# Paired bilinear products: x turned by disjoint pairs, part of w in place, five blocks of x through GpSimd's queue

## The chip, the cores and the metric

The kernel runs on one core of a Trainium2 chip. A core has a matrix engine (TensorE, PE), a vector engine (VectorE, DVE), a scalar engine (ScalarE, ACT), a general engine (GpSimd, POOL) and a queue engine (SyncE, SP). They share an on-chip memory of 128 partitions; PE writes its results to a second, small one, PSUM. Sixteen DMA engines move data between the on-chip memory and HBM; transfers are issued from the queues of SP, ACT and POOL.

The metric is the device time of one execution in microseconds (us), lower is better. The kernel before takes 1345.69 us, the median of 9 runs from 1344.93 to 1346.57.

## The reference

```python
# inputs: (4096, 32, 64) float32; W: (496, 64, 64) float32
idx_i, idx_j = np.triu_indices(F, k=1)      # the 496 pairs i < j of 32 fields
vi = inputs[:, idx_i, :]
vj = inputs[:, idx_j, :]
vidots = jnp.einsum('bpd,pde->bpe', vi, W)
return vidots * vj                          # (4096, 496, 64) float32
```

For each row of the batch and each pair (i, j), field i is multiplied by the pair's own 64x64 matrix and the result, element by element, by field j. The output has 520 MB; x has 33.6 MB and W 8.1 MB.

## The kernel before

**Tiles.** The 4096 rows form 16 blocks of 256; a block has two tiles of 128 rows, one row to a partition (two neighbouring rows of the batch share a partition, one for each tile). The list `steps` goes through the fields i, and for each i through its pairs in chunks of at most 16 (`CH`). The pairs are cut into five groups by `bounds`; a group's results for a tile are gathered in one tile `ot` of a pool of three buffers, and one SP transfer (L266) writes it to HBM, some 3 MB. The first group of the first tile goes out in two transfers.

**A step.** PE needs x with its elements across partitions. `turn_x` (L138) turns eight windows of two neighbouring fields each: window s holds fields s - 1 and s, so that each field comes up twice, once in each half of the partitions. ACT copies the result from PSUM to `xT` (L147, 128x1024). The matrices W are taken in two halves h of 32 columns: two matmuls (L244), one from each half of the partitions, fill the two banks of a tile `ps`. A step that crosses a bound of `wrows` (multiples of 128 pairs) needs two more. Then DVE multiplies `ps` by field j and writes `ot` (L261). For the first chunk of the fields in `aside`, ACT copies `ps` to `tmp` (L258) and POOL multiplies (L259).

**W.** It is loaded in four parts of 128, 128, 128 and 112 pairs (`load_w`, L113) to tiles `raw`. `order_w` (L120) sorts a quarter of a part on DVE, POOL or ACT into a tile `rp` of the pool that `tmp` uses, PE turns it (`turn_w`, L127), and ACT copies it to the part's own tile `wT`. The first two parts' `raw` use buffers of `ot`; parts three and four use, one after the other, a buffer of their own. Part four is loaded by ACT's queue after the last `order_w` of part three (L231).

**The order of the work.** It is written out in the program. The first three tiles (`LEAD`) go through the groups together, the others one by one (`sched`). The dictionary `due` puts turns of x four steps (`AHEAD`) before the step that needs them, and the work on W at fixed steps. In steps 52 to 66 (`no_aside`) no product goes to ACT and POOL.

**Loads of x.** SP loads block 0 in two halves, with W's first three parts and block 1 (L193 to L200). Later blocks are loaded one block ahead, into two buffers. `new_x` (L69) takes the buffer and has POOL clear one field at its front (L72). Then ACT's queue loads 128 rows of 16 KB (`load_x`), except for blocks 4, 7, 10 and 13: `load_fifteen` (L95) loads 120 rows by two transfers from POOL's queue, in pieces of 4 KB, and the last 8 rows by two transfers from ACT's queue (5 rows and 3). After each of POOL's two comes a transfer of 17 rows of a few bytes (`turn_engines`, L86); one of 5 rows stands at the start and one of 11 at the end.

Of the kernel before, what the change touches and what calls it, by code (L numbers as in the profile page):

```python
# [8 lines left out]
F32 = mybir.dt.float32  # L9
# [3 lines left out]
def kernel(  # L13
# [16 lines left out]
    nc = tc.nc  # L30

    B, F, D = x.shape
    P = 128
    NB = 2
    assert 2 * D == P and B % (NB * P) == 0
    NBLK = B // (NB * P)
    NP = F * (F - 1) // 2
    E2 = D // 2
    BANK = 512
    CH = BANK // E2  # L40
    RUN = 2 * BANK // P
    p0 = [i * (F - 1) - i * (i - 1) // 2 for i in range(F)]


# [4 lines left out]
    aside = (1, 3, 5, 7, 9, 11, 13)  # L49

    cuts = [*range(0, NP, P), NP]
    wrows = list(zip(cuts[:-1], cuts[1:]))

    const = ctx.enter_context(tc.tile_pool(name="const", bufs=1))
    xpool = ctx.enter_context(tc.tile_pool(name="xpool", bufs=2))
    xtpool = ctx.enter_context(tc.tile_pool(name="xtpool", bufs=4))
    tpool = ctx.enter_context(tc.tile_pool(name="tpool", bufs=4))
    opool = ctx.enter_context(tc.tile_pool(name="opool", bufs=3))
    psum = ctx.enter_context(tc.tile_pool(name="psum", bufs=4, space=bass.MemoryType.PSUM))

    ident = const.tile([P, P], F32, tag="ident", name="ident")
    make_identity(nc, ident)

    xs = {}

    def rows_of(dram: bass.AP, blk: int) -> bass.AP:
        return dram[blk * NB * P : (blk + 1) * NB * P]

    def new_x(blk: int):  # L69

        xs[blk] = xpool.tile([P, 1 + NB * F, D], F32, tag="xs", name=f"xs_{blk}")
        nc.gpsimd.memset(xs[blk][:, 0, :], 0.0)  # L72

    def load_x(blk: int, eng, k0: int = 0, k1: int = NB):
        src = rows_of(x, blk).rearrange("(p k) f d -> p (k f) d", k=NB)
        eng.dma_start(out=xs[blk][:, 1 + k0 * F : 1 + k1 * F, :], in_=src[:, k0 * F : k1 * F, :])

# [1 line left out]
    SWR = 120  # L81
# [4 lines left out]
    def turn_engines(k: int):  # L86
        n = k if k > 1 else 17
        c = used[0] % 8
        used[0] += 1
        src = x[: NB * n].rearrange("(p k) f d -> p k f d", k=NB)  # L90
        tc.keep_in_program_order(
            nc.gpsimd.dma_start(out=scratch[:n, :, c : c + 1], in_=src[:, :, 0, 0:1])  # L92
        )

    def load_fifteen(blk: int):  # L95
        rows = rows_of(x, blk).rearrange("(p k) f d -> p k f d", k=NB)
        dst = xs[blk][:, 1:, :].rearrange("p (k f) d -> p k f d", k=NB)
        for a, b in ((SWR, SWR + 5), (SWR + 5, P)):
            nc.scalar.dma_start(out=xs[blk][a:b, 1:, :], in_=rows[a:b].rearrange("p k f d -> p (k f) d"))
        for h in range(2):  # L100
            cut = slice(h * F // 2, (h + 1) * F // 2)
            tc.keep_in_program_order(
                nc.gpsimd.dma_start(out=dst[:SWR, :, cut, :], in_=rows[:SWR, :, cut, :])  # L103
            )
            turn_engines(1)


    wflat = w.rearrange("p d e -> p (d e)")
    raw, wT = {}, {}
    EU = 2 * BANK // P  # L110
    NU = E2 // EU

    def load_w(c: int, eng=nc.sync):  # L113

        a, b = wrows[c]
        pool, tag = ((opool, "ot"), (opool, "ot"), (const, "w3"), (const, "w3"))[c]
        raw[c] = pool.tile([P, D * D], F32, tag=tag, name=f"raw_{c}")
        eng.dma_start(out=raw[c][: b - a, :], in_=wflat[a:b])

    def order_w(c: int, k: int, copy):  # L120
        r = wrows[c][1] - wrows[c][0]
        rp = tpool.tile([P, EU, 2, D], F32, tag="tmp", name=f"rp_{c}_{k}")
        src = raw[c][:r, :].rearrange("p (d h e) -> p e h d", h=2, d=D)
        copy(rp[:r], src[:, k * EU : (k + 1) * EU])  # L124
        return rp

    def turn_w(c: int, k: int, rp, copy):  # L127
        r = wrows[c][1] - wrows[c][0]
        if c not in wT:
            wT[c] = const.tile([P, r, E2], F32, tag=f"w{c}", name=f"wT_{c}")  # L130
        pt = psum.tile([P, EU, P], F32, tag="ps", name=f"ptw_{c}_{k}")
        for n in range(EU):
            nc.tensor.transpose(  # L133
                pt[:, n, :r], rp[:r, n].rearrange("p h d -> p (h d)"), ident[:r, :r]
            )
        copy(wT[c][:, :, k * EU : (k + 1) * EU], pt[:, :, :r].rearrange("p e r -> p r e"))  # L136

    def turn_x(blk: int, k: int, q: int, copy):  # L138

        pt = psum.tile([P, RUN, P], F32, tag="ps", name=f"ptx_{blk}_{k}_{q}")  # L140
        for n in range(RUN):
            s = k * F + q * RUN + n
            nc.tensor.transpose(  # L143
                pt[:, n, :], xs[blk][:, s : s + 2, :].rearrange("p f d -> p (f d)"), ident
            )
        xT = xtpool.tile([P, RUN, P], F32, tag="xT", name=f"xT_{blk}_{k}_{q}")
        copy(xT, pt)  # L147
        return xT


# [8 lines left out]
    first = {}  # L159
# [11 lines left out]
    place = {ts: n for n, ts in enumerate(sched)}  # L171


    AHEAD = 4
    due: dict = {}
    for t in range(NT):
        for q in range(F // RUN):
            at = place[t, first[q * RUN - 1] if q else 0] - AHEAD
            due.setdefault(max(0, at), []).append(("x", t // NB, t % NB, q))
    for c, orders, turns in (  # L180
        (1, (2, 4, 8, 10), (4, 7, 12, 15)),
        (2, (17, 22, 27, 32), (19, 24, 29, 34)),
        (3, (54, 54, 55, 55), (57, 60, 63, 66)),
    ):
        for k in range(NU):
            due.setdefault(orders[k], []).append(("order", c, k))
            due.setdefault(turns[k], []).append(("turn", c, k))
    no_aside = range(52, 67)
    LATE = 6
    loads = {place[blk * NB, LATE]: blk + 1 for blk in range(2, NBLK - 1)}  # L190
    loads[place[LEAD, LATE]] = 2
# [3 lines left out]
    load_w(0)  # L195
    load_w(1)
    load_x(0, nc.sync, 1, NB)
    load_w(2)
    new_x(1)
    load_x(1, nc.sync)  # L200
    turn_engines(5)

    v, p, a = nc.vector.tensor_copy, nc.gpsimd.tensor_copy, nc.scalar.copy
# [9 lines left out]
    for s, (t, st) in enumerate(sched):  # L213
        blk, kt = divmod(t, NB)
        g, i, c0, m = steps[st]
        if s in loads:
            new_x(loads[s])
            if loads[s] % 3 == 1:
                load_fifteen(loads[s])
            else:  # L220
                load_x(loads[s], nc.scalar)
        for what, *args in due.get(s, ()):
            if what == "x":
                xT[tuple(args)] = turn_x(*args, a)
            elif what == "turn":
                turn_w(*args, rps.pop(tuple(args)), a)
            else:
                c, k = args
                rps[c, k] = order_w(c, k, (v, v, p, v)[c] if k % 2 == 0 else (v, v, p, a)[c])
                if (c, k) == (2, NU - 1):  # L230
                    load_w(3, nc.scalar)  # L231

        base, end = groups[g]
        pa = p0[i] + c0
        if pa == base:
            ots[t] = opool.tile([P, cap, D], F32, tag="ot", name=f"ot_{t}_{g}")
        ot = ots[t]
        ps = psum.tile([P, 2, CH, E2], F32, tag="ps", name=f"ps_{s}")
        for c, (lo, hi) in enumerate(wrows):
            lo, hi = max(pa, lo), min(pa + m, hi)  # L240
            if lo < hi:
                for h in range(2):
                    n = i + 1 - h
                    nc.tensor.matmul(  # L244
                        ps[:, h, lo - pa : hi - pa, :],
                        xT[blk, kt, n // RUN][h * D : (h + 1) * D, n % RUN, :],
                        wT[c][h * D : (h + 1) * D, lo - wrows[c][0] : hi - wrows[c][0], :],
                        start=True,
                        stop=True,
                    )  # L250
        o = pa - base
        j = 1 + kt * F + i + 1 + c0
        dst = ot[:, o : o + m, :].rearrange("p m (h e) -> p m h e", h=2)
        src = ps[:, :, :m, :].rearrange("p h m e -> p m h e")
        xj = xs[blk][:, j : j + m, :].rearrange("p m (h e) -> p m h e", h=2)
        if i in aside and c0 == 0 and s not in no_aside:
            tmp = tpool.tile([P, CH, 2, E2], F32, tag="tmp", name=f"tmp_{s}")
            nc.scalar.copy(tmp, src)  # L258
            nc.gpsimd.tensor_mul(dst, tmp, xj)  # L259
        else:  # L260
            nc.vector.tensor_mul(dst, src, xj)  # L261

        ends = (p0[2], end) if s < NS and (t, g) == (0, 0) else (end,)
        if pa + m in ends:
            n0 = p0[2] if len(ends) > 1 and pa + m == end else base
            nc.sync.dma_start(  # L266
                out=rows_of(out, blk).rearrange("(p k) n d -> p k n d", k=NB)[:, kt, n0 : pa + m, :],
                in_=ot[:, n0 - base : pa + m - base, :],
            )
# [28 lines left out]
```

## Time and profile before

| | before |
|---|---|
| median of 9 runs | 1345.69 us |
| profiled execution: time, span | 1344.93 us, 1343.1 us |
| busy: PE, DVE, POOL, ACT | 1160.6, 956.2, 544.9, 374.1 us |
| moved by DMA | 562.95 MB, 419 GB/s on average |
| HBM read, written | 41.68 MB, 520.09 MB |
| median time from issue to landing: output transfers | 16.3 to 17.1 us |
| the same: x by ACT's queue, x by POOL's queue | 17.8, 31.5 us |
| mean granted clock of TensorE | 0.963 |

The span runs from the first instruction to the last on the core; the execution's time is a little longer. Busy time is the sum of an engine's instructions. In a row of a stretch of time, the columns are the stretch, its length, the busy time of PE, PE's weight loads, DVE, ACT and POOL (with counts), the granted clock, the mean busy share of the 16 DMA engines, and GB/s. In a row of waits, they are who waited for whom, the total in us, how often, and the longest.

### The profile page before, as it was taken

How to read it: one execution, taken by the hardware profiler on the slowest of the kernel's cores; microseconds unless marked ns; L12 is line 12 of the kernel's file. 1: busy time of each engine (PE TensorE's matmuls, PEld its weight loads, DVE VectorE, ACT ScalarE, POOL GpSimd, SP SyncE). 2: the span in 40 equal slices, each digit the busy share in tenths (PEclk: the TensorE clock that was granted, in tenths of full speed). 3: DMA queues.
4: the chain of work that ended last, by engine and by line, in shares of the span. 5: the costliest groups of instructions: out<-in, count | busy, mean ns of one | idle time of the engine just before them, and what ended most of it. 6: DMA issues, size and time to landing. Idle time of an engine off the chain costs nothing.

```text
span 1343.1 us, 17902 instructions
## 1 busy us (share of the span) xinstructions
PE 1160.6 (86%) x7424; PEld 677.1 (50%) x7424; DVE 956.2 (71%) x1262; ACT 374.1 (28%) x367; POOL 544.9 (41%) x264
## 2 busy tenths in 40 slices
PE   6989889888898888888889988888988889889894
PEld 4555545544455444455545554444554445545552
DVE  5778768766677677776757777576876667767774
ACT  3432322223232232222222322232222323223321
POOL 1822424444243445333444434442444424344431
PEclk9989999999999899998989999899899989989997
DMA  9999999999999999999999999999999999999997
GB/s 394 376 422 420 422 426 432 428 418 432 423 431 422 431 430 399 428 424 432 429 418 419 413 428 430 425 426 416 418 423 414 430 420 431 420 430 424 423 418 319
DMA packets 28258, 562.95 MB, mean 419 GB/s; under 512 B 3456, under 2 KB 3456, under 8 KB 5504
## 3 DMA queue, kind: packets, MB, share of 16 engines
q1 hardware_dynamic: 24048, 530.59, 93.0%
q10 hardware_dynamic: 1632, 23.33, 4.2%
q0 software_dynamic: 2496, 7.88, 1.5%
q8 instruction: 58, 0.95, 0.3%
q14 instruction: 24, 0.20, 0.0%
HBM read 41.68 MB, written 520.09 MB: 418 GB/s over the span
## 4 chain that ended last, share of the span: by engine, by line
DMA 52%; PE 22%; DVE 15%; POOL 6%; issue 2%; ACT 1%; DVEq 0%; SPq 0%; POOLq 0%; ACTq 0%
DMA out_dram<-ot 51%; PE ps L244 17%; DVE ot L261 15%; POOL ot L259 5%; PE ptx L143 4%; PE ptw L133 1%; DMA raw<-in_L_rec_W_dram 1%; POOL scratch L92 1%; ACT tmp L258 1%; POOL xs L103 0%; DVE rp L124 0%; POOL rp L124 0%; DVEq L261 0%; ACT wT L136 0%; POOL xs L72 0%
## 5 line engine op out<-in xcount | busy, mean ns | idle before, releaser
L261 DVE TENSOR_TENSOR ot<-ps,xs 128x1024 f32<-128x1024 f32 (+15 forms) x1252 | 944.9, 809 | 356.1 <-DMA out_dram<-ot 193.0
L244 PE MATMUL ps<-wT,xT 64*128 64x512 f32 (+13 forms) x6272 | 1015.6, 466 | 122.3 <-DVE ot L261 110.3
L244 PEld LDWEIGHTS ps<-wT,xT 64*128 64x128 f32 x6272 | 550.9, 193 | 552.7 <-DVE ot L261 291.0
L259 POOL TENSOR_TENSOR ot<-tmp,xs 128x1024 f32<-128x1024 f32 x220 | 519.3, 2361 | 621.0 <-ACT tmp L258 441.3
L258 ACT COPY tmp<-ps 128x1024 f32<-128x1024 f32 x220 | 222.8, 1013 | 465.9 <-PE ps L244 388.4
L147 ACT COPY xT<-ptx 128x1024 f32<-128x1024 f32 x128 | 129.6, 1012 | 453.6 <-PE ptx L143 453.6
L143 PE MATMUL ptx<-ident,xs 128*128 128x128 f32 x1024 | 141.2, 281 | 38.5 <-DVE ot L261 29.8
L143 PEld LDWEIGHTS ptx<-ident,xs 128*128 128x128 f32 x1024 | 111.1, 142 | 85.1 <-issue 42.2
L72 POOL MEMSET xs<- 128x64 f32 x16 | 2.4, 151 | 148.9 <-DVE ot L261 148.9
L133 PE MATMUL ptw<-ident,rp 128*128 128x128 f32 (+1 forms) x128 | 18.0, 292 | 3.9 <-DVE rp L124 3.9
L136 ACT COPY wT<-ptw 128x1024 f32<-128x1024 f32 (+1 forms) x15 | 14.8, 984 | 20.3 <-PE ptw L133 20.3
L133 PEld LDWEIGHTS ptw<-ident,rp 128*128 128x128 f32 (+1 forms) x128 | 15.1, 153 | 10.3 <-DVE rp L124 5.0
L124 DVE COPY rp<-raw 128x1024 f32<-128x1024 f32 (+1 forms) x9 | 10.7, 1217 | 11.2 <-DMA raw<-in_L_rec_W_dram 11.2
L92 POOL DMA_DIRECT2D scratch<-in_r_inputs_dram x10 | 9.1, 908 | 0.2 <-issue 0.2
L124 POOL COPY rp<-raw 128x1024 f32<-128x1024 f32 x4 | 7.9, 1981 | 0.1
L124 ACT COPY rp<-raw 112x1024 f32<-112x1024 f32 (+1 forms) x3 | 5.9, 1953 | 4.6 <-POOL ot L259 2.8
L103 POOL DMA_DIRECT2D xs<-in_r_inputs_dram x8 | 6.0, 753 | 1.4 <-issue 1.4
L136 DVE COPY wT<-ptw 128x1024 f32<-128x1024 f32 x1 | 1.2, 1225 | 2.4 <-PE ptw L133 2.4
L147 ACT ACT_TABLE_LOAD x1 | 1.3, 1283 | 0.7 <-PEq L285 0.7
masks.py:197 POOL MEMSET ident<- 128x128 f32 x1 | 0.2, 204 | 0.3 <-POOLq L285 0.3
masks.py:199 POOL TENSOR_SCALAR_AFFINE_SELECT ident<-ident 128x128 f32<-128x128 f32 x1 | 0.3, 287 | 0.0
L285 POOL MEMSET const-float32-0.0<- 128x1 f32 x1 | 0.1, 93 | 0.3 <-issue 0.3
(3 smaller groups left out, 0.3 us busy)
## 6 DMA issues: line engine op xcount, KB each, us to landing
out_dram<-ot SPq DMA_DIRECT2D x64, 3360.0 KB, 16.3
out_dram<-ot SPq DMA_DIRECT2D x32, 3168.0 KB, 16.4
out_dram<-ot SPq DMA_DIRECT2D x32, 3104.0 KB, 17.0
out_dram<-ot SPq DMA_DIRECT2D x31, 2880.0 KB, 17.1
xs<-in_r_inputs_dram ACTq DMA_DIRECT2D x10, 2048.0 KB, 17.8
xs<-in_r_inputs_dram POOLq DMA_DIRECT2D x8, 960.0 KB, 31.5
raw<-in_L_rec_W_dram SPq DMA_DIRECT2D x3, 2048.0 KB, 17.5
xs<-in_r_inputs_dram SPq DMA_DIRECT2D x2, 1024.0 KB, 5.5
```

Source lines behind the costliest of these rows:

```text
L72: nc.gpsimd.memset(xs[blk][:, 0, :], 0.0)
L92: nc.gpsimd.dma_start(out=scratch[:n, :, c : c + 1], in_=src[:, :, 0, 0:1])
L103: nc.gpsimd.dma_start(out=dst[:SWR, :, cut, :], in_=rows[:SWR, :, cut, :])
L124: copy(rp[:r], src[:, k * EU : (k + 1) * EU])
L133: nc.tensor.transpose(pt[:, n, :r], rp[:r, n].rearrange("p h d -> p (h d)"), ident[:r, :r])
L136: copy(wT[c][:, :, k * EU : (k + 1) * EU], pt[:, :, :r].rearrange("p e r -> p r e"))
L143: nc.tensor.transpose(pt[:, n, :], xs[blk][:, s : s + 2, :].rearrange("p f d -> p (f d)"), ident)
L147: copy(xT, pt)
L244: nc.tensor.matmul(ps[:, h, lo - pa : hi - pa, :], xT[blk, kt, n // RUN][h * D : (h + 1) * D, n % RUN, :], wT[c][h * D : (h + 1) * D, lo - ...
L258: nc.scalar.copy(tmp, src)
L259: nc.gpsimd.tensor_mul(dst, tmp, xj)
L261: nc.vector.tensor_mul(dst, src, xj)
```

## The change

Six things change together:

- `turn_x` turns eight fields by four disjoint windows of two fields, so a tile takes 16 transposes, not 32. ACT makes three copies of the result: all 128 partitions to the first half of `xT`, and each half of the partitions to the other half, in the second half of `xT`. The field at the front of a block's tile, and POOL's clearing of it, go. A block's tile now has 16 spare elements after each row, so ACT's loads come in pieces of 8 KB.
- The first three parts of W share one tile for 384 pairs (`home_of`); no step is split at 128 or 256 any more. The third part is loaded straight into its place in this tile and sorted from there.
- The fourth part of W is loaded by SP at the start, after block 1 and the third part. Block 1 now comes before the third part.
- Blocks 3, 6, 9, 12 and 15 go through POOL's queue: 120 rows in one transfer of 8 KB pieces, one of 17 short rows, then the last 8 rows in two transfers, each with half of the fields.
- x is turned six steps ahead, not four; W's third and fourth parts are sorted and turned at other steps.
- `no_aside` goes; in the first three tiles ACT copies `ps` to `ot` itself and POOL multiplies in place.

```diff
-    RUN = 2 * BANK // P
+    RUN = 8
...
-        xs[blk] = xpool.tile([P, 1 + NB * F, D], F32, tag="xs", name=f"xs_{blk}")
-        nc.gpsimd.memset(xs[blk][:, 0, :], 0.0)
+        wide = xpool.tile([P, NB, F * D + 16], F32, tag="xs", name=f"xs_{blk}")
+        xs[blk] = wide[:, :, : F * D].rearrange("p k (f d) -> p k f d", d=D)
...
-        for a, b in ((SWR, SWR + 5), (SWR + 5, P)):
-            nc.scalar.dma_start(out=xs[blk][a:b, 1:, :], in_=rows[a:b].rearrange("p k f d -> p (k f) d"))
+        def part(ps: slice, fs: slice):
+            tc.keep_in_program_order(nc.gpsimd.dma_start(out=dst[ps, :, fs, :], in_=rows[ps, :, fs, :]))
+
+        part(slice(0, SWR), slice(0, F))
+        turn_engines(1)
         for h in range(2):
-            cut = slice(h * F // 2, (h + 1) * F // 2)
-            tc.keep_in_program_order(
-                nc.gpsimd.dma_start(out=dst[:SWR, :, cut, :], in_=rows[:SWR, :, cut, :])
-            )
-            turn_engines(1)
+            part(slice(SWR, P), slice(h * F // 2, (h + 1) * F // 2))
...
+    def home_of(c: int):
+        home, tag, n = (wrows[3][0], "w3", NP - wrows[3][0]) if c == 3 else (0, "w", wrows[3][0])
+        if home not in wT:
+            wT[home] = const.tile([P, n, E2], F32, tag=tag, name=f"wT_{home}")
+        return wT[home][:, wrows[c][0] - home : wrows[c][1] - home, :]
...
+        if c == 2:
+            raw[c] = home_of(c).rearrange("p r e -> p (r e)")
...
-        for n in range(RUN):
-            s = k * F + q * RUN + n
+        for u in range(RUN // 2):
+            f = q * RUN + 2 * u
             nc.tensor.transpose(
-                pt[:, n, :], xs[blk][:, s : s + 2, :].rearrange("p f d -> p (f d)"), ident
+                pt[:, u, :], xs[blk][:, k, f : f + 2, :].rearrange("p f d -> p (f d)"), ident
             )
-        copy(xT, pt)
+        copy(xT[:, 0], pt)
+        copy(xT[D:, 1], pt[:D])
+        copy(xT[:D, 1], pt[D:])
...
-    AHEAD = 4
+    AHEAD = 6
...
-        (2, (17, 22, 27, 32), (19, 24, 29, 34)),
-        (3, (54, 54, 55, 55), (57, 60, 63, 66)),
+        (2, (16, 18, 25, 27), (30, 33, 36, 39)),
+        (3, (46, 48, 50, 52), (56, 59, 62, 65)),
...
-    load_w(2)
     new_x(1)
     load_x(1, nc.sync)
+    load_w(2)
+    load_w(3)
...
-            if loads[s] % 3 == 1:
+            if loads[s] % 3 == 0:
                 load_fifteen(loads[s])
...
-                if (c, k) == (2, NU - 1):
-                    load_w(3, nc.scalar)
...
-        if i in aside and c0 == 0 and s not in no_aside:
-            tmp = tpool.tile([P, CH, 2, E2], F32, tag="tmp", name=f"tmp_{s}")
+        if i in aside and c0 == 0:
+
+            tmp = dst
+            if t >= LEAD:
+                tmp = tpool.tile([P, CH, 2, E2], F32, tag="tmp", name=f"tmp_{s}")
```

## The prediction

> **What bounds the kernel now.** I read the page's slices first, then its chain of waits, then the stretches of the span where the transfer rate falls short.
>
> ```profile
> PE 1160.6 (86%) x7424; PEld 677.1 (50%) x7424; DVE 956.2 (71%) x1262; ACT 374.1 (28%) x367; POOL 544.9 (41%) x264
> ...
> DMA  9999999999999999999999999999999999999997
> ...
> q0 software_dynamic: 2496, 7.88, 1.5%
> ...
> DMA out_dram<-ot 51%; PE ps L244 17%; DVE ot L261 15%; POOL ot L259 5%; PE ptx L143 4%; PE ptw L133 1%; DMA raw<-in_L_rec_W_dram 1%; POOL scratch L92 1%; ACT tmp L258 1%; POOL xs L103 0%; DVE rp L124 0%; POOL rp L124 0%; DVEq L261 0%; ACT wT L136 0%; POOL xs L72 0%
> ```
>
> No compute engine is full; the 16 DMA engines are, in every slice but the last. The output transfers carry half of the chain. So the time is 563 MB over the rate, plus what the rate loses, and a change of compute is worth only what it does to the DMA. The second view, busy time by stretch, shows where rate is lost (last columns: DMA share, GB/s):
>
> ```profile
> 2.00:26.00 24.00, 14.56 (x82) 10.54 (x84) 10.97 (x11) 9.09 (x9) 2.64 (x2) 1.00 1.00 419
> 26.00:36.00 10.00, 10.00 (x58) 5.25 (x56) 8.51 (x9) 4.05 (x4) 3.85 (x3) 1.00 0.88 368
> 36.00:56.00 20.00, 20.00 (x122) 11.29 (x118) 14.64 (x15) 9.29 (x10) 16.42 (x9) 1.00 0.95 404
> 56.00:64.00 8.00, 8.00 (x56) 5.20 (x56) 5.41 (x6) 4.09 (x5) 5.88 (x3) 1.00 0.99 318
> 64.00:92.00 28.00, 23.43 (x152) 15.27 (x149) 20.84 (x25) 11.36 (x10) 7.54 (x4) 0.88 1.01 432
> 92.00:104.00 12.00, 11.95 (x86) 7.47 (x86) 9.83 (x14) 4.36 (x5) 4.02 (x2) 1.00 0.93 396
> ...
> 140.00:500.00 360.00, 314.32 (x2012) 181.87 (x2012) 257.76 (x344) 99.22 (x98) 152.30 (x71) 0.97 1.00 428
> 500.00:520.00 20.00, 17.90 (x119) 10.11 (x116) 16.60 (x23) 4.05 (x4) 7.79 (x8) 1.00 0.98 397
> 520.00:690.00 170.00, 146.97 (x943) 84.66 (x943) 120.98 (x160) 46.57 (x46) 69.55 (x32) 0.97 1.00 425
> ...
> 920.00:960.00 40.00, 32.56 (x192) 18.55 (x188) 24.82 (x30) 10.12 (x10) 16.63 (x8) 0.91 0.98 412
> 960.00:1180.00 220.00, 192.69 (x1246) 110.92 (x1246) 160.69 (x216) 60.75 (x60) 92.17 (x45) 0.98 1.00 423
> 1180.00:1320.00 140.00, 126.09 (x802) 73.61 (x798) 102.48 (x136) 39.48 (x39) 60.93 (x27) 0.95 1.00 424
> ```
>
> The full rate is 430 to 432. Three things are lost against 430. First, the start: 10 x (1 - 368/430) = 1.4 us, 20 x (1 - 404/430) = 1.2, 8 x (1 - 318/430) = 2.1 and 12 x (1 - 396/430) = 0.9, together 5.7 us. PE is busy throughout 26 to 64: there the DMA waits for compute. Second, from 500 us on the rate is some 1% lower than in 140 to 500. Third, the end, by the same view in steps of 2 us:
>
> ```profile
> 1332.00:1334.00 2.00, 0.00 (x0) 0.00 (x0) 0.00 (x0) 0.00 (x0) 0.00 (x0) 0.50 1.00 430
> 1334.00:1336.00 2.00, 0.00 (x0) 0.00 (x0) 0.00 (x0) 0.00 (x0) 0.00 (x0) 0.50 0.13 54
> 1336.00:1338.00 2.00, 0.00 (x0) 0.00 (x0) 0.00 (x0) 0.00 (x0) 0.00 (x0) 0.50 0.06 27
> 1338.00:1340.00 2.00, 0.00 (x0) 0.00 (x0) 0.00 (x0) 0.00 (x0) 0.00 (x0) 0.50 0.06 27
> ```
>
> A share of 0.06 is one engine of 16: fifteen are done at about 1334.5, one works on alone for 6 us. The trace's completion marks (16 for each output transfer) say the same all along. The last engine ends this far behind the median one: 1.3 us at 158, 3.4 at 263, 1.8 at 287, 3.3 at 396, 6.2 at 502, 3.0 at 551, 6.9 at 764, 3.3 at 797, 6.9 at 1011, 3.2 at 1060, 6.6 at 1333. Between 396 and 502 the lag grows by 2.9 us in 106, or 2.7%: one engine is that much slower. It falls by about 3.5 us after the four loads through GpSimd's queue (issued at 264, 511, 756, 1003). With three output buffers the other fifteen run out of work once the lag is near 6 us; that is the loss after 500 us.
>
> **What the Trainium skill says.** "DMA: Bandwidth & Descriptors", section "Why a DMA increments its semaphore by 16 and not by 1": a transfer runs on the largest k up to 16 that divides its outermost dimension, and GpSimd's queue puts a k below 16 on consecutive engines from a cursor that goes round. So 120 rows take 15 engines and leave one out, and the tiny transfers at L92 set the cursor. The trace agrees: 1920 packets of 4 KB for eight such loads, 240 each, 16 on each of 15 engines, and the lag falls each time. The same page, section "Issuing engines are not separate DMA queues": whichever queue issues, the same 16 engines move the bytes. The trace agrees: w's fourth part on ACT's queue at 55 us slows the outputs beside it (318 GB/s). The page's section "Bandwidth" gives a ceiling of 435 GB/s; this trace reaches 432, so the steady rate has no more to give.
>
> **The change part by part.** All sums are against the profiled execution (span 1343.1 us, its time 1344.93); its distance to the median, 0.76 us, I carry over.
>
> *Relief of the slow engine.* Before, in each of four blocks a fast engine moves 8 rows of 16 KB in 32 pieces of 0.159 us (the trace's packet), 5.1 us, and the spared one gets one row by ACT's queue, 0.6: relief 4.5, in all 18 us. After, in each of five blocks a fast engine moves 8.5 rows, and the spared one half a row: 16 x 0.309 + 2 x 0.159 = 5.3 against 0.3, relief 4.9, in all 24.7 us. From about 190 us to the end the slow engine always lags, so always has work; the time can fall by no more than the 6.7 us more that are taken from it, plus what it idled at the start. The five loads come at about 180, 427, 673, 920 and 1165 (where those blocks load now). The lag then runs: 1.4 to -3.4 at 180, +6.6 per 247 us, so 3.2 at 427, 5 at 673, 6.8 at 920, 6.5 at 1165, some 6 at the end. It is over 5.5 us for about 115 us instead of 300. The excess loss after 500 us is, against 430 GB/s, 14.1 us in 820, less 3.8 at the rate of 140 to 500: 10 us. Of this the shorter time at the limit saves up to 6. I take 4.5, bounds 0 and 6.7. The end keeps its tail.
>
> *Start.* The first line of SP's queue now also holds w's fourth part (1.79 MB, 4.2 us at 430), ahead of the first output. It fills the gap of 26 to 36, keeps the queue fed in 36 to 56 and takes the mixed stretch 56 to 64 away. DVE and ACT then need not wait for it: in the chain it is waited for until 74.3, and the gap of 92 to 104 follows from that and from a drop of the PE clock to 0.57 at 76 to 84. Compute is quicker there too: each x transpose group has 4 transposes fewer, 4 x 0.138 us, and two turns of w's third part (1.1 us each) move behind the first three outputs. What becomes late: the first output lands some 4 us later (about 38 us), and with it the buffer for the fifth output; compute reaches that point by 38 to 42, so a stall of 0 to 1 us, under a full DMA queue. Of the 5.7 us I take 4.5; bounds 2 and 5.7.
>
> *One more block through GpSimd's queue.* The 50 us with such a load run at 422 (260 to 310) and 410 (500 to 550): 0.9 and 2.3 us lost, part of it the lag's; a load by ACT costs about 0.5. I add 0.5 us, bounds 0 and 1.5. POOL's issues at 0.75 us each, four a block, stand behind the wait for the x buffer. What is queued behind them is POOL's multiplies; the memset waited in the same place for all 14 blocks:
>
> ```profile
> POOL xs L72 <- DVE ot L261: 148.9, 14, 18.3
> ```
>
> Now only five blocks make POOL wait, and ACT's load waits itself, as it did behind the memset.
>
> *Pieces of 8 KB.* By ACT, 2 x 0.309 against 0.611 us: 7 ns x 8 rows x 9 blocks = +0.5 us an engine. By GpSimd 9 ns x 80 pieces = -0.7. They cancel.
>
> *Compute.* PE loses 512 transposes at 0.138 us, 71 us, and 128 split matmuls. ACT gets two copies of 64x512 and one of 128x512 for one of 128x1024 at 1.01 us; no row has them. They cost between 0.5 (half) and 1.0 us each, so +0.5 to +2 us a group, 64 to 256 us in all, on an engine busy 28%. With six steps of lead over PE instead of four, nothing waits. All of this is hidden by the DMA, nothing in steady state; without that cover ACT's worst case would be 630 us, still under PE. Reading w's third part in its final place makes its turns wait for all four orders; they stand 3 to 12 steps apart. PE's instructions are fetched in 16 KB pieces by the same DMA engines: 1536 records fewer, 6 pieces x 0.6 us / 16 = -0.2.
>
> Sum: -4.5 - 4.5 + 0.5 + 0 - 0.2 = -8.7; I round the gain down to 8.2 for the clock drop, which may come again: 1345.7 - 8.2 = 1337.5.
>
> **The rivals.** *Only the start gains.* The block order 3, 6 .. 15 relieves the slow engine first when its lag is 1.4 us, where it is worth nothing, and the extra load costs its 1.5: then -4.5 + 1.5 to -4.5, 1341 to 1343. For it: at 140 to 260 nothing is lost at 430 GB/s. Against: a lead is kept, since the queue holds two outputs. *Nothing gains.* The start's compute keeps its pace (PE, DVE and POOL carry the chain up to 130 us), gaps only move later, and the extra load eats the rest: 1344 to 1346. *Slower:* the two 8-row transfers move the cursor otherwise than by 16 a block, and the load of 120 rows spares another engine than the slow one. Then the slow engine gets all its work back: 18 us, less the 4.5 of the start, 1355 to 1360. It decides from the third load on, where the lag would pass 6 us. Against it: 8 rows give k = 8, twice 8 is 16, and 15 + 1 is 16.
>
> **How the numbers follow.** Both gains 0.64 (1333 to 1341), only the start 0.16, nothing 0.10, slower 0.10. The range 1331.5 to 1345 takes in the bounds of the first (-12.6 at best, -0.7 at worst) and the second rival. A difference of 0.2%, 2.7 us, is about what a measurement of this kernel can tell from none; with part of the second rival inside it: faster 0.79, same 0.10, slower 0.11.
>
> **What would show it.** Start right: 26 to 64 us at 425 GB/s or more, no wait for raw after 40 us. Relief right: the lag falls by 4 to 5 us after five loads, and seldom reaches 6. Cost of the load: 50 us stretches at 410 to 422. Wrong: one engine's lag growing past the loads, rates below 420 over long stretches, or output transfers waiting for POOL or ACT.

## The result, and the profile after

The changed kernel takes 1339.07 us, the median of 9 runs from 1337.62 to 1339.68. Beside it the kernel before took 1345.72 us (29 runs, 1344.61 to 1346.98). The ratio is 0.9948, with a 95% interval of 0.9940 to 0.9956: 6.65 us faster, where 8.2 were forecast. The profiled execution took 1339.1 us with a span of 1337.3.

From the page of the changed kernel, its busy times, the slices of the DMA, GpSimd's queue and the chain of waits:

```profile
PE 1129.0 (84%) x6656; PEld 596.4 (45%) x6656; DVE 951.0 (71%) x1258; ACT 471.7 (35%) x627; POOL 552.5 (41%) x256
...
DMA  9999999999999999999999999999999999999997
...
q0 software_dynamic: 2064, 10.50, 2.0%
...
DMA out_dram<-ot 55%; PE ps L254 19%; DVE ot L274 15%; POOL ot L272 3%; PE ptx L154 2%; DMA xs<-in_r_inputs_dram 1%; ACT tmp L271 1%; DVE rp L134 0%; PE ptw L143 0%; ACT xT L158 0%; ACT xT L159 0%; ACT xT L160 0%; DVEq L274 0%; POOL xs L100 0%; POOL rp L134 0%
```

The kernel stands where it stood: the DMA is full in every slice but the last, and output transfers carry half of the chain. PE lost 32 us of work and ACT gained 98, and neither is seen in the time. (The working took 71 us from PE for the transposes. They fell by 57, from 141.2 to 84.4, and the product matmuls rose by 23, from 1015.6 to 1038.3.) The stretches of the span, with the columns as before (the last two are the DMA share and GB/s):

```profile
2.00:26.00 24.00, 13.39 (x72) 9.44 (x72) 10.22 (x9) 10.55 (x13) 2.99 (x2) 1.00 0.99 418
26.00:36.00 10.00, 9.07 (x50) 4.58 (x48) 9.63 (x9) 4.78 (x6) 2.36 (x1) 1.00 1.01 330
36.00:56.00 20.00, 19.69 (x108) 10.23 (x110) 16.28 (x17) 7.39 (x8) 16.50 (x8) 1.00 1.01 434
56.00:64.00 8.00, 8.00 (x52) 4.84 (x50) 5.31 (x6) 6.31 (x8) 6.83 (x4) 1.00 0.99 421
64.00:92.00 28.00, 24.52 (x160) 13.65 (x158) 21.71 (x25) 17.82 (x20) 15.42 (x8) 1.00 1.00 428
92.00:104.00 12.00, 12.00 (x90) 7.19 (x92) 9.66 (x15) 6.58 (x10) 8.91 (x4) 1.00 1.03 439
...
140.00:500.00 360.00, 309.04 (x1790) 162.78 (x1786) 256.83 (x339) 124.89 (x168) 154.29 (x71) 0.95 1.00 426
500.00:520.00 20.00, 17.68 (x108) 8.93 (x105) 15.69 (x22) 6.53 (x9) 6.87 (x3) 1.00 1.00 415
520.00:690.00 170.00, 143.38 (x836) 74.75 (x834) 119.89 (x160) 57.42 (x78) 71.48 (x34) 0.95 1.00 424
...
920.00:960.00 40.00, 32.45 (x194) 17.03 (x192) 26.59 (x38) 13.06 (x18) 19.28 (x11) 0.96 1.01 415
960.00:1180.00 220.00, 187.36 (x1096) 97.06 (x1094) 158.20 (x208) 76.16 (x102) 94.38 (x43) 0.97 1.00 424
1180.00:1320.00 140.00, 121.92 (x736) 64.00 (x732) 104.56 (x144) 48.74 (x66) 57.62 (x26) 0.98 1.00 428
```

Three things are to be seen. The gaps of the start are gone: from 36 to 104 the DMA share is 0.99 to 1.03 and the rate is 421 or more, where it was 318 to 432. But the stretch 26 to 36 is slower than before, 330 GB/s against 368, and now with a share of 1.01: the engines are busy and slow. And the steady part has changed little: 426 instead of 428 up to 500 us, and 415 to 428 after it, where it was 397 to 425.

Counted from the bytes of the trace's packets, without the rounding of these rows, the start up to 140 us is 3.9 us shorter, and the rest 1.9 us, 1.3 of it up to 1320. The two make up the 5.8 us between the two profiled executions. So the start paid about what was expected and the relief of the slow engine half. Within the rest, 500 to 1320 us loses 11.3 us against 430 GB/s instead of 14.2, but 140 to 500 loses 3.7 instead of 2.1. Every profile of the new code below loses more than before in this stretch (2.7 to 6.6 us), and no run says why.

The end is as long as it was, though one engine is alone (a share of 0.06 is one of 16) only for the last 2 to 3 us of it:

```profile
1330.00:1332.00 2.00, 0.00 (x0) 0.00 (x0) 0.00 (x0) 0.00 (x0) 0.00 (x0) 0.50 0.16 67
1332.00:1334.00 2.00, 0.00 (x0) 0.00 (x0) 0.00 (x0) 0.00 (x0) 0.00 (x0) 0.50 0.06 27
1334.00:1336.00 2.00, 0.00 (x0) 0.00 (x0) 0.00 (x0) 0.00 (x0) 0.00 (x0) 0.50 0.03 13
```

Three words for what follows. A transfer's 16 completion marks say when each engine was done with its part; the *lag* is the time from their median to the last one; a *relief* is a load of 120 rows, which leaves one engine out. The marks don't name the engines. The lag in the changed kernel was 1.6 us at 71, 3.1 at 118, 3.6 at 179, then 1.6 at 220, 6.2 at 425, 3.1 at 466, 7.0 at 678, 3.4 at 711, 7.5 at 924, 4.5 at 966, 7.6 at 1170, 4.3 at 1204, 6.3 at 1336. It falls after each of the five loads through GpSimd's queue, by 2.0, 3.1, 3.6, 3.0 and 3.3 us.

### The profile page after: what moved, and what is told of

It is laid out like the page before. It is cut to its first block, busy times and chain, and to the rows that moved or that the text cites. A ratio compares the mean times of both kernels' runs of the same rounds, so it can differ in the third digit from the quotient of the medians.

```text
span 1337.3 us, 16689 instructions
## 1 busy us (share of the span) xinstructions
PE 1129.0 (84%) x6656; PEld 596.4 (45%) x6656; DVE 951.0 (71%) x1258; ACT 471.7 (35%) x627; POOL 552.5 (41%) x256
## 4 chain that ended last, share of the span: by engine, by line
DMA 56%; PE 21%; DVE 15%; POOL 3%; issue 2%; ACT 1%; DVEq 0%; SPq 0%; POOLq 0%; ACTq 0%
DMA out_dram<-ot 55%; PE ps L254 19%; DVE ot L274 15%; POOL ot L272 3%; PE ptx L154 2%; DMA xs<-in_r_inputs_dram 1%; ACT tmp L271 1%; DVE rp L134 0%; PE ptw L143 0%; ACT xT L158 0%; ACT xT L159 0%; ACT xT L160 0%; DVEq L274 0%; POOL xs L100 0%; POOL rp L134 0%
## 5 line engine op out<-in xcount | busy, mean ns | idle before, releaser
L254 PE MATMUL ps<-wT,xT 64*128 64x512 f32 (+13 forms) x6016 | 1038.3, 484 | 174.4 <-DVE ot L274 169.7
L254 PEld LDWEIGHTS ps<-wT,xT 64*128 64x128 f32 x6016 | 527.2, 193 | 626.7 <-DVE ot L274 388.4
L272 POOL TENSOR_TENSOR ot<-tmp,xs 128x1024 f32<-128x1024 f32 x203 | 479.0, 2360 | 706.9 <-ACT tmp L271 519.2
L271 ACT COPY tmp<-ps 128x1024 f32<-128x1024 f32 x203 | 205.5, 1012 | 467.7 <-PE ps L254 432.0
L158 ACT COPY xT<-ptx 128x512 f32<-128x512 f32 x128 | 75.0, 586 | 331.2 <-PE ptx L154 331.2
L154 PE MATMUL ptx<-ident,xs 128*128 128x128 f32 x512 | 84.4, 288 | 10.2 <-DMA xs<-in_r_inputs_dram 6.7
L154 PEld LDWEIGHTS ptx<-ident,xs 128*128 128x128 f32 x512 | 53.9, 141 | 82.3 <-DVE ot L274 58.8
L160 ACT COPY xT<-ptx 64x512 f32<-64x512 f32 x128 | 74.6, 582 | 1.6
L159 ACT COPY xT<-ptx 64x512 f32<-64x512 f32 x128 | 73.9, 577 | 1.5
L272 POOL TENSOR_TENSOR ot<-ot,xs 128x1024 f32<-128x1024 f32 x21 | 50.0, 2385 | 51.0 <-ACT ot L271 50.9
L271 ACT COPY ot<-ps 128x1024 f32<-128x1024 f32 x21 | 21.3, 1013 | 24.6 <-PE ps L254 19.4
L134 DVE COPY rp<-raw 128x1024 f32<-128x1024 f32 (+1 forms) x9 | 14.7, 1651 | 10.8 <-DMA raw<-in_L_rec_W_dram 10.8
## 6 DMA issues: line engine op xcount, KB each, us to landing
xs<-in_r_inputs_dram POOLq DMA_DIRECT2D x5, 1920.0 KB, 24.9
```

The costliest lines, as they stand in the source:

```text
L134: ins = copy(rp[:r], src[:, k * EU : (k + 1) * EU])
L154: nc.tensor.transpose(pt[:, u, :], xs[blk][:, k, f : f + 2, :].rearrange("p f d -> p (f d)"), ident)
L158: copy(xT[:, 0], pt)
L159: copy(xT[D:, 1], pt[:D])
L160: copy(xT[:D, 1], pt[D:])
L254: nc.tensor.matmul(ps[:, h, lo - pa : hi - pa, :], xT[blk, kt, i // RUN][h * D : (h + 1) * D, (i + h) % 2, i % RUN // 2, :], wT[home][h * ...
```

## The experiments

Each is an edit of the changed kernel, timed in five rounds beside the kernel before, which took 1345.7 to 1346.0 us on the same chips. Differences are against the changed kernel's 1339.07.

**No load of 120 rows.** ACT's queue loads all blocks whole, so every engine moves the same share of x.

```diff
-            if loads[s] % 3 == 0:
+            if False:
```

> The changed kernel, but no block of x goes through GpSimd's queue; all come by ScalarE's, 16 engines each. If one engine is slow and the loads of 120 rows spare just it, it gets 5 x 4.9 = 24.7 us of work back: +18 to +24 us over the changed kernel (1339.1), 1357 to 1363, with the last engine 6 to 8 us behind the others from about 200 us on and the mean DMA share below 1. Rival (the gain is the start's alone, the order of the blocks is worth nothing): within 2 us of 1339.

Measured: 1349.45 us (8 runs, 1349.16 to 1350.14), ratio 1.0028 (1.0017 to 1.0038). The relief is worth 10.4 us. That is real, and half of what my theory gave it. The marks show a limit: the lag grows to about 7 us by 450 us and then stays between 6.1 and 7.4 (up to 8.9 beside a load of x), one engine some 5 us behind the next. The rate over the long stretch as one row, in the kernel before:

```profile
500.00:1320.00 820.00, 717.84 (x4586) 415.54 (x4582) 591.66 (x785) 223.74 (x221) 343.07 (x163) 0.97 1.00 423
```

The same stretch in the changed kernel:

```profile
500.00:1320.00 820.00, 698.51 (x4116) 364.40 (x4112) 589.50 (x792) 281.42 (x380) 339.35 (x153) 0.97 1.00 424
```

And without the loads of 120 rows:

```profile
500.00:1320.00 820.00, 701.13 (x4078) 368.59 (x4079) 584.21 (x780) 281.26 (x380) 330.02 (x141) 0.95 0.99 420
```

From 424 to 420 is 820 x 4 / 430 = 7.6 us of the 10.4. Counted from the bytes, this stretch loses 19.0 us against 430 GB/s, or 2.3% of its length, near the 2.7% by which the prediction found one engine to be slower. That fits: once the lag is at its limit, all engines would move at about the pace of the slow one. One GB/s in this row is 1.9 us, so it carries large differences and not small ones: that before stands at 423 and after at 424 says only that the two are near.

**Another engine spared.** The short transfers at the start and the end are changed by one row, which moves the cursor of GpSimd's queue by one engine for the whole run; everything else is the same. Once down, once up.

```diff
-    turn_engines(5)
+    turn_engines(4)
...
-    turn_engines(11)
+    turn_engines(12)
```

> The changed kernel, but the first tiny transfer has 4 rows and the last 12, so that the cursor stands one engine lower and the loads of 120 rows spare the engine before the slow one. If it is one certain engine that is slow: no relief, as much as without GpSimd's queue, 1357 to 1363, or somewhat more as the slow engine takes 8.5 rows. If any engine spared would do: 1339.

> The changed kernel, but the first tiny transfer has 6 rows and the last 10: the cursor stands one engine higher. If one engine alone is the slow one, sparing the engine above it is as bad as sparing the one below (1352.8): 1350 to 1354. If the engine above is slow too: 1340 to 1347.

(The second has 6 and 10 rows.) Measured: 1352.81 us (5 runs, 1352.44 to 1353.18), ratio 1.0050 (1.0038 to 1.0063), and 1353.36 us (5 runs, 1352.66 to 1353.47), ratio 1.0055 (1.0043 to 1.0067). The first one's long stretch:

```profile
500.00:1320.00 820.00, 700.20 (x4060) 368.26 (x4060) 582.55 (x778) 280.55 (x380) 336.26 (x151) 0.95 0.99 418
```

So one certain engine is to be spared, and the changed kernel spares it: a cursor off by one, to either side, costs 13.7 and 14.3 us and makes the kernel slower than before. Sparing the wrong engine is 3.4 to 3.9 us worse than sparing none, so the loads through GpSimd's queue aren't better in themselves. These two runs are also what shows that a load of 120 rows leaves one engine out: the prediction's 240 packets to a load would fit 15 on each of 16 engines as well. By the packets of the prediction, each load then gives the slow engine 5.3 us instead of 16 x 0.309 = 4.9, 1.6 us in five loads; the rest, some 2 us, would be what five such loads cost in themselves, an estimate by subtraction that takes each us of the slow engine for one of the kernel.

**Four loads, and seven.** The first has blocks 4, 7, 10 and 13 through GpSimd's queue, the kernel before's choice. The second has 3, 5, 7, 9, 11, 13 and 15.

```diff
-            if loads[s] % 3 == 0:
+            if loads[s] % 3 == 1:
```

```diff
-            if loads[s] % 3 == 0:
+            if loads[s] % 2 == 1:
```

> The changed kernel, but blocks 4, 7, 10 and 13 through GpSimd's queue as before, not 3, 6 .. 15. If relief is worth its full size where the lag is at its limit: one load fewer, up to 4.9 us, 1341 to 1344. If a fifth load costs what it brings: 1338.5 to 1339.5.

> The changed kernel, but blocks 3, 5 .. 15, seven of them, through GpSimd's queue. If the slow engine still sets the pace late in the run: two reliefs more take away the 2 us of idle engines and most of the last engine's tail, -2 to -5 us, 1334 to 1337. If the loads by GpSimd's queue cost 1 us each more than by ScalarE's and the lag costs little: 1339 to 1341.

Measured: four, 1340.88 us (5 runs, 1340.73 to 1341.58), ratio 0.9963 (0.9951 to 0.9976); seven, 1334.18 us (4 runs, 1333.59 to 1335.10), ratio 0.9913 (0.9899 to 0.9926). Five loads at 3, 6 .. 15 instead of four at 4, 7 .. 13 are worth 1.8 us, with intervals that overlap a little; two more are worth 4.9. The long stretch with seven:

```profile
500.00:1320.00 820.00, 709.08 (x4120) 374.96 (x4116) 591.44 (x792) 281.24 (x380) 344.88 (x161) 0.94 1.00 426
```

So the slow engine still set the pace in the changed kernel. How late the last engine was tells the same. This table is counted from the completion marks of the output transfers, one execution of each kernel; the share is that of the transfers after 140 us:

| kernel | median lag, 500 to 1315 us | share with a lag over 5.5 us | time |
|---|---|---|---|
| before | 5.2 us | 0.30 | 1345.7 |
| no load of 120 rows | 6.9 | 0.82 | 1349.5 |
| another engine spared (one row fewer) | 6.8 | 0.85 | 1352.8 |
| four loads | 6.2 | 0.49 | 1340.9 |
| changed kernel, five | 5.9 | 0.47 | 1339.1 |
| seven | 4.4 | 0.11 | 1334.2 |

The large steps go with the time: with no relief, or a wrong one, the lag is at its limit, and seven loads take 1.5 us off that of five. The small ones are within the scatter: the profiles of four more kernels with the same five loads, described below, have medians of 4.8 to 5.5. The kernel before has less lag than the changed kernel and more time, since its start loses more.

**The last part of W loaded as 128 rows.** Sixteen pairs of the third part are loaded a second time, so that the transfer has 128 rows instead of 112; the rows that are there already are left out when PE's result is copied.

```diff
         a, b = wrows[c]
+        if c == 3:
+            a = b - P
...
-        r = wrows[c][1] - wrows[c][0]
+        r = P
+        o = P - (wrows[c][1] - wrows[c][0])
...
-        copy(home_of(c)[:, :, k * EU : (k + 1) * EU], pt[:, :, :r].rearrange("p e r -> p r e"))
+        copy(home_of(c)[:, :, k * EU : (k + 1) * EU], pt[:, :, o:].rearrange("p e r -> p r e"))
```

> The changed kernel, but the last part of W is loaded with 128 rows, 16 of which are loaded twice, not with 112. If a load of 112 rows is slow in itself (its packets of 16 KB took 0.88 us on average against 0.61 in the loads ahead of it): 2.1 MB at 430 GB/s, 4.9 us, against 1.8 MB at 290, 6.3 us; the stretch 26 to 36 reads 420 GB/s or more and the time falls by 1 to 2 us to 1337 to 1338. If the slowness is that of the time (outputs beside it, compute): packets stay at 0.88 us, +1 us.

Measured: 1337.55 us (5 runs, 1336.65 to 1337.78), ratio 0.9941 (0.9927 to 0.9954): the median is 1.5 us lower, though 0.26 MB more are moved, but this interval overlaps the changed kernel's (0.9940 to 0.9956). The trace is clearer. The stretch that was 330 GB/s:

```profile
26.00:36.00 10.00, 8.89 (x48) 4.49 (x48) 9.64 (x9) 4.78 (x6) 2.36 (x1) 1.00 1.01 400
```

The DMA alone from 28 to 34 us, when the load of this part is under way, in the changed kernel (packets, bytes, rate):

```profile
DMA packets 120, 1.72 MB, mean 287 GB/s; under 512 B 14, under 2 KB 14, under 8 KB 14
```

The same six us with 128 rows:

```profile
DMA packets 155, 2.24 MB, mean 374 GB/s; under 512 B 16, under 2 KB 16, under 8 KB 16
```

The trace's packets of 16 KB took 0.61 us in the loads of 128 rows ahead of it. In the load of 112 rows none was that quick, and the mean is 0.93 us (the 0.88 of the expectation had the last packets of the load ahead mixed in). With 128 rows 92 of the packets took 0.62 us, but the other 36, nearly all between 29 and 32 us, took 0.93. Against 430 GB/s the stretch loses 0.7 to 1.0 us in the three profiles with 128 rows, here and below, and 2.0 to 2.3 in six with 112. So most of what is lost in the 330 goes with the 112 rows; why the end of the longer load is slow too stays open, and the 420 GB/s that was expected wasn't reached. The Trainium skill, "SBUF — State Buffer", section "Door 1: The DMA port swizzle", says that a transfer's rate depends on how many of 16 memory ports its partitions reach, and which partitions share one. By its formula 112 rows give twelve ports eight rows each and four ports four; if the ports set the pace, an estimate is 112 / 128 x 430 = 376 GB/s. The trace has 287, lower than that, so the ports' load alone doesn't explain it, and no run here shows which engine wrote which rows.

**The last part of W loaded later.** The load goes back to where the kernel before had it, behind the third part's last `order_w`, on ACT's queue. First in the plain way:

```diff
-    load_w(3)
...
+                if (c, k) == (2, NU - 1):
+                    load_w(3, nc.scalar)
```

> The changed kernel, but the last part of W is loaded by ScalarE's queue after the third part has been sorted, as in the kernel before. If the early load is what fills the start: the gap at 30 to 36 us comes back, PE waits for the part near 60 to 75 us, +1.5 to +4 us, 1340.5 to 1343. If the start's gain comes from PE's fewer transposes and the order of the other work: 1339 to 1340.

Measured: 1346.13 us (13 runs, 1344.02 to 1347.48), ratio 1.0001 (0.9993 to 1.0009), 7.1 us slower. But it wasn't the experiment that I meant. Nothing held the transfer back, since its buffer is free from the start, and the trace shows it issued at 0.7 us, beside the first loads. Two stretches of the start:

```profile
2.00:26.00 24.00, 6.12 (x36) 5.52 (x36) 4.19 (x4) 7.22 (x8) 0.30 (x1) 1.00 0.99 357
...
36.00:56.00 20.00, 18.75 (x102) 9.48 (x101) 18.60 (x18) 7.51 (x9) 10.94 (x6) 1.00 0.80 337
```

The slow transfer now shares the engines with W's first parts and x, on which all compute waits: DVE waits 18.6 us for its first `raw`, against 10.8, and what is late there comes back as a gap at 36 to 56. It shows what the place of such a load is worth. The second attempt keeps the load in its place on the queue:

```diff
+        ins = eng.dma_start(out=raw[c][: b - a, :], in_=wflat[a:b])
+        if c == 3:
+            tc.keep_in_program_order(ins)
```

> The changed kernel, but the last part of W by ScalarE's queue after the third part's last sort, and held at that place in ScalarE's program (in the run with the late load it went out at 0.7 us, beside the first loads). If the early load fills the start: the gap near 30 to 36 us comes back, part four is waited for at 60 to 70 us, +1.5 to +4 us over 1339.1, 1340.5 to 1343. If the early load is worth nothing: 1338.5 to 1339.5.

Measured: 1341.88 us (7 runs, 1341.33 to 1343.55), ratio 0.9972 (0.9961 to 0.9982), 2.8 us slower. The load is issued at 48.4 us, and the gaps of the kernel before are back:

```profile
26.00:36.00 10.00, 9.34 (x52) 4.58 (x48) 9.64 (x9) 4.78 (x6) 2.36 (x1) 1.00 0.80 336
36.00:56.00 20.00, 19.42 (x106) 10.29 (x108) 16.54 (x17) 8.28 (x9) 16.18 (x8) 1.00 0.92 347
56.00:64.00 8.00, 8.00 (x52) 4.81 (x50) 4.94 (x5) 5.45 (x7) 7.03 (x4) 1.00 0.96 395
```

A share of 0.80 and 0.92 is idle DMA: 10 x 0.20 + 20 x 0.08 = 3.6 us, about the 2.8 measured. The early load earns its gain by filling a time in which compute has no output to hand over yet. The wait for part four that was expected at 60 to 70 us didn't come: nothing waits for a `raw` after the first sort. Nor is there a gap from 92 to 104 us, where the rate is 430.

**Twice as many transposes of x.** Each is issued twice, the second writing the same result again, which gives PE back the 512 that the change took away.

```diff
-            nc.tensor.transpose(
+            for _ in range(2):
+              nc.tensor.transpose(
```

> The changed kernel, but each transpose of x is made twice, so that a tile has 32 again (the same result is written twice). If the transposes are hidden under the DMA: +0 to +1.5 us, all of it in the first 100 us, 1339 to 1340.5. If PE's lead is worth something all along: 71 us of PE more, +3 us or more.

Measured: 1340.90 us (5 runs, 1340.82 to 1341.57), ratio 0.9967 (0.9954 to 0.9979), 1.8 us slower, with intervals that just overlap. The long stretches keep their rate, 426 from 140 to 500 us and 424 from 500 to 1320, though PE does 31 us more work in the second of them. Of the start, the stretch 26 to 36 falls to 316. In steady state PE's transposes are hidden. At the start they may be worth up to some 2 us; by its trace, this kernel loses 4.0 us from 26 to 140 us, within the 2.9 to 4.4 of kernels without the second transposes.

**Both improvements, and nine loads.** The load of 128 rows with seven blocks, and with nine (3, 5, 7, 8, 10, 11, 13, 14, 15).

```diff
-            if loads[s] % 3 == 0:
+            if loads[s] in (3, 5, 7, 8, 10, 11, 13, 14, 15):
```

> Both: the last part of W with 128 rows, and seven blocks through GpSimd's queue. If the two losses lie at different places they add up: 1332 to 1336. If what one frees the other loses again: no faster than the better of the two.

> The last part of W with 128 rows, and nine blocks (3, 5, 7, 8, 10, 11, 13, 14, 15) through GpSimd's queue. If the spared engine still lags with seven: 1331 to 1333.5. If other engines set the pace by then, and each load costs them about 0.5 us more than ScalarE's: 1334 to 1336, no better than with seven (1333.7).

Measured: seven, 1333.72 us (4 runs, 1332.96 to 1337.19), ratio 0.9917 (0.9903 to 0.9931); nine, 1335.54 us (6 runs, 1333.08 to 1339.64), ratio 0.9930 (0.9916 to 0.9943). Seven with 128 rows is the fastest median here, 12.0 us under the kernel before, but not told apart from seven alone; the two gains alone would sum to 6.4 and are 5.3 together. Nine loads lower the median lag to 3.7 us and bring nothing more. A second engine is about as late by then: already in the changed kernel the last two engines end within 0.03 to 1 us of each other after each relief. From 951 to 989 us the lag stays at 4.5 while the last but one comes up from 1.3 to 0.1 us ahead of the last; after that the lag grows again, to 6.3 at 1079. That fits a last engine that falls no further behind until the slow one comes up with it, but the marks don't say which is which.

## Why the prediction was right, and where it was not

*Start, forecast -4.5.* The mechanism was right. Unrounded, the start gained 3.9 us in the profiled execution. Six profiles of kernels with the same start lose 2.9 to 4.4 us against 430 GB/s from 26 to 140, where before lost 6.7, so 2.3 to 3.8 is the better reading of this term. The loaded queue fills 36 to 56 (434), and the gap of 92 to 104 is gone in this execution (439), though in two of the six it stood at 411. Putting the load back costs 2.8; the transposes account for up to 1.8, and the two overlap. The sign that the prediction named, 425 GB/s or more from 26 to 64 us, was met in the middle only (330, 434, 421).

Two readings of the kernel before were wrong here. The prediction has the wait for part four last until 74.3 us. The chain shows an output transfer in that place, and then DVE, busy with a product before it sorts:

```profile
57.67 15.82 DMA out_dram<-ot
73.68 0.61 issue
74.29 2.60 DVE rp L124
```

The load had landed by 69.7 us, and nothing waited for a `raw` after the first sort before the change either, so no such wait was saved. Nor did the gap of 92 to 104 follow from the late load: the kernel that puts it back has none.

The other is the reading of 56 to 64. I put its 318 GB/s down to a load mixed in between outputs, or to a DMA that waits for compute, and took the stretch as "taken away". But its DMA share was 0.99, and a load that only shares the engines leaves the sum as it is: the kernel before has 430 GB/s from 140 to 260 us, a load of x on ACT's queue among its outputs. It is the load of 112 rows that is slow, wherever it stands: its packets took 0.82 us on average there, 0.93 in the changed kernel, 0.91 beside the first loads and 0.81 when it was put back. It moved to 26 to 36, and that stretch still loses 10 x (1 - 330/430) = 2.3 us. The sum took 4.2 us for it, at 430; six us at 287 GB/s show that price to be too low.

*Relief of the slow engine, forecast -4.5, with +0.5 for the extra load.* The mechanism was right: two kernels that spare a neighbour lose 14 us, one that spares nobody loses 10.4, one with two more loads gains 4.9. The size was not: 140 us to the end gained 1.9, not 4.0. The term that failed is the path of the lag. I had it at 1.4 us at 180, 4.9 off at each load, and over 5.5 us for about 115 us in all, so that it would seldom reach 6. It was 3.6 at 179, 2.0 to 3.6 came off, and 47% of the outputs after 140 us had more than 5.5, 38% more than 6.

Three things went into this. First, a slip in the sum: 6.8 at 920, less 4.9, plus 6.6, is 8.5 at 1165 and not 6.5, if no limit on the lag is brought in. Second, by the marks another engine seems to be the last one after a relief, so a relief shows less than its size. The prediction's own list had a sign of this: the first load of the kernel before took off 1.6 us, from a lag of 3.4, and not the 3.5 it gives for all four; the last two engines then ended together. Third, the lag at the start of the path was higher, and this scatters: at about 178 us, ahead of any relief, six profiles with the same start have 1.2 to 3.6 us, and the kernel whose start has its gaps back has 2.7 at 174. So the runs don't show that the full start made it so. The kernel that puts back four loads at the old blocks gives 1.8 for the fifth load and the new blocks together, about what 140 us to the end gained.

*No relief would cost 18 us.* This price stood in the rival of a slower kernel. With other engines spared the cost is 13.7 and 14.3 us against the changed kernel, so the rival's time would have been 1353 and not 1355 to 1360, and the expectations of 1357 to 1363 for no relief and for another engine were too high as well. By the bytes, the kernel without relief loses no more than the changed one from 140 to 500 us, 4.0 us against 3.7, while its lag grows; then it loses 19.0 against 11.3. The rival didn't occur since the cursor was right, by the sum that the prediction gives (16 engines a block).

*The extra load, pieces of 8 KB.* Not told apart. GpSimd's loads landed in 24.9 us, against 31.5 before.

*Compute hidden.* Right. The unknown copies, from the page's groups:

```profile
L158 ACT COPY xT<-ptx 128x512 f32<-128x512 f32 x128 | 75.0, 586 | 331.2 <-PE ptx L154 331.2
...
L160 ACT COPY xT<-ptx 64x512 f32<-64x512 f32 x128 | 74.6, 582 | 1.6
L159 ACT COPY xT<-ptx 64x512 f32<-64x512 f32 x128 | 73.9, 577 | 1.5
```

They take 0.58 us each, near the lower bound of 0.5, whether they have 128 partitions or 64. The group costs 1.75 us against 1.01, 94 us in all, on an engine at 35%. PE's instruction fetches fell from 58 packets to 52, the six that were foretold.

*The end* kept its tail, 6.3 us for the last engine. But it was alone for only the last 2.3 of them, where the one before was alone for some 6.

Of the rivals, "only the start gains" (1341 to 1343) came nearer to the parts than to the time: most of the gain is the start's, but the relief did pay, and 1339.07 lies 2 us below it.

Two things stay open. Which engine is slow, and why by 2.7%, no run settles: the trace of the kernel before has an instruction fetch of 16 KB every 23 us, its packet 0.96 us on average, and an estimate from the two is 4% of one engine that had to do them all; that is of the size needed, and was not shown. And why moving some 23 us of work back to that engine costs 10.4 us and not 23 is answered in part only: a lag below its limit of 6 to 7 us costs little, and without relief that limit is reached only at 450 us, and a second engine is close behind. That the three output buffers set the limit is argued and not tested.

## What to carry to other kernels

Where the DMA is full, look at how far its last engine is behind, transfer by transfer: giving one engine less to do was worth 10.4 us here, where 32 us less of PE's work were not seen, and sparing the wrong engine cost 14, so test both neighbours and the number of such loads. Fill the DMA's early gaps with loads that are needed later anyway, but place them behind what the first compute waits for. And price a transfer by its own packets in the trace, not by the kernel's steady rate.

## What the runs showed of the hardware that was not expected

A load of 112 rows of 16 KB ran at 287 GB/s with all engines busy, its packets 0.93 us instead of 0.61; with 16 rows too many the same six us moved 374 GB/s, and the kernel's median was 1.5 us lower, with intervals that overlap. One certain DMA engine of the 16 falls behind, by some 2.7% in the kernel before, and to spare the neighbour on either side doesn't help (13.7 and 14.3 us more). ACT's copy out of PSUM takes as long for 64 partitions as for 128, 0.58 us for 512 elements each.
